# Tiles of 128 rows for remainders in the second expert layer, and its first tile's first layer placed at the end of the attention before it

## The chip, the core and the metric

The kernel runs on one core of one Trainium2 chip. The metric is the device time of one execution in microseconds; three executions are timed, and a further one is recorded by the profiler. All arithmetic is in 32-bit floats.

The engines are named as in the profile: PE is TensorE's matrix products and PEld its weight loads, DVE is VectorE, ACT is ScalarE, POOL is GpSimd, SP is SyncE, which here only issues transfers. Each engine works off its own queue in order.

## What is computed

Two decoder layers follow one another. Each has a cross-attention and a mixture of experts, and each result is added to its input. The part that matters here is the last step, the second mixture of experts:

```python
x = x + _L0_xattn_ref(...)
x = x + _L0_ffn_ref(...)
x = x + _L1_xattn_ref(ctx_1024, _layernorm(x), Wq, Wk, Wv, 1, 0, 1)
x = x + _L1_ffn_ref(_layernorm(x), W1, b1, W2, b2, Wr, br)

def _L1_ffn_ref(x, W1, b1, W2, b2, Wr, br):
    xf = x.reshape(-1, D)                    # 2048 rows of 256
    logits = xf @ Wr + br                    # 8 experts
    topv, _ = lax.top_k(logits, 2)
    masked = jnp.where(logits >= topv[:, 1:2], logits, -jnp.inf)
    weights = jax.nn.softmax(masked, axis=-1)
    h = gelu(jnp.einsum('td,edh->eth', xf, W1) + b1[:, None, :])   # 256 -> 1024
    expert_out = jnp.einsum('eth,ehd->etd', h, W2) + b2[:, None, :]  # 1024 -> 256
    return jnp.einsum('etd,te->td', expert_out, weights)
```

Each of the 2048 rows (4 batches of 512) has a weight of zero for all but its two best experts, so the kernel computes only those 4096 pairs of row and expert.

## The kernel before

The kernel gathers the rows of each expert and works on them in tiles of `G` = 256 rows, `GR` = 2 blocks of `P` = 128. A row that has been routed is scattered, together with its number and its weights (`PAY` = 265 values), into a table in DRAM. There are two such tables. `rows_a` has exactly 256 places for each expert and takes rows of the first three batches; `rows_b` takes what overflows there, and all rows of the last batch. Which rows fall to which expert is known only when the kernel runs. So the first eight tiles, one for each expert, come from `rows_a` at fixed addresses (`first_tile`, L1591). Further tiles come from `rows_b` by indirect gathers, whose indices the kernel works out itself (`table`, L1683; `further_tile`, L1750). `SURE` = 13 such tiles are always done. More of them, up to 21 in all, are written out behind conditions on a counter (`beyond`, L1826), and one of these is fetched in advance.

**A tile.** `turned` (L1613) transposes the 256 rows on TensorE into `tp` and copies them to `xT` with VectorE. `hidden` (L1623) is the first layer: 16 products of 128 by 128 by 256 in four groups, each group followed by two GELUs on ScalarE into `hT`. `second` (L1647) and `results` (L1673) are the second layer: for each block of 128 rows 8 products into `ps_y`, a multiplication by the row's weight on VectorE into `y`, and an indirect add into the output in DRAM by GpSimd (`add_out`, L1661). `told` (L1570) reads from the gathered rows where each row goes (`to`) and its weight (`share`). The tiles `to`, `share` and `y` come from the pool `five`, which has five buffers of each; a sixth use waits until the add that reads the first is done. In the profile each product of 32-bit floats shows as two records.

**The order of tiles.** The loop at L1801 does `hidden` of tile i, fetches tile i + 2, does `turned` and `told` of tile i + 1, then `results` of tile i - 1. Between these it takes steps of `rest`, a generator that routes the last batch (`route2`, L396) and then works out the tables. These are the source's order only: in this stage a scheduler at build time decides the order on each engine. The weights of an expert are 4104 values for each partition, 2052 KB. There are four places for them, chosen by `room` (L1579): the large tile `cw`, the pool `new`, and two buffers of the pool `kv1`.

**Before that stage** comes the second cross-attention, which has 16 units of 13 tiles of keys each, in steps of two tiles. There `in_order` fixes the order of the source on every computing engine, and a table `at`, filled by `put`, says which other work is issued at which step. `closing` (L1396) ends a unit: copy of the result `oT`, row sums over the adds `sum` (`ps_n`, then the copy `by`), transposes (`tp_o`), and the add into `x`. In the last batch the routing of the third batch runs beside it, with its scatters into `rows_a` and `rows_b` on GpSimd. `load_first_weights` (L1448) fetches the weights of tiles 0, 1 and 2 in this stage; `cw` takes those of tile 2. The pools of the expert stage reuse the memory of the attention's, so its first operations wait for the attention's last ones, the scatters included.

The lines that the loop and the places of weights rest on:

```python
        def room(k):
            if k % 4 == 2:
                return cw[:, :WIDE]
            if k % 4 == 3:
                return new.tile([P, WIDE], F32, tag="w", name="w_e")
            return kv1.tile([P, KV], F32, tag="kv", name="w_e")[:, :WIDE]
```

Of the kernel before, what the change touches and what calls it, by code (L numbers as in the profile page):

```python
# [8 lines left out]
F32 = mybir.dt.float32  # L9
# [7 lines left out]
P = 128  # L17
# [39 lines left out]
SURE = 13  # L57
# [13 lines left out]
def xattn_ffn_twice(ctx: ExitStack, tc: tile.TileContext, a: dict, out: bass.AP):  # L71
# [1243 lines left out]


# [3 lines left out]
    with ExitStack() as st:  # L1320
# [127 lines left out]
        def load_first_weights():  # L1448
# [11 lines left out]
            nc.sync.dma_start(cw[:, :WIDE], a["wall"][2 * P : 3 * P, :])  # L1460
# [6 lines left out]
            first_weights.append(lambda i, n: cw[:, i : i + n])  # L1467
# [44 lines left out]
        put(per_batch * (B - 1) + 4, load_first_weights)  # L1512

# [44 lines left out]
    with ExitStack() as st:  # L1558
# [4 lines left out]
        five = st.enter_context(tc.tile_pool(name="d_five", bufs=5))  # L1563
# [6 lines left out]
        def told(rows, share_of):  # L1570

            to = five.tile([P, GR], I32, tag="to", name="to")
            share = five.tile([P, GR], F32, tag="share", name="share")
            for r in range(GR):
                nc.vector.tensor_copy(to[:, r : r + 1], rows[r][:, D : D + 1])
                share_of(share[:, r : r + 1], rows[r][:, D + 1 :])
            return rows, to, share

        def room(k):  # L1579


            if k % 4 == 2:
                return cw[:, :WIDE]
            if k % 4 == 3:
                return new.tile([P, WIDE], F32, tag="w", name="w_e")
            return kv1.tile([P, KV], F32, tag="kv", name="w_e")[:, :WIDE]
# [4 lines left out]
        def first_tile(e):  # L1591

            rows = []
            for r in range(GR):
                got = three.tile([P, PAY], F32, tag=f"rows{r}", name=f"rows{r}")
                nc.sync.dma_start(got, rows_a[e * G + r * P : e * G + (r + 1) * P, :])
                rows.append(got)
# [15 lines left out]
        def turned(rows, two=two):  # L1613

            xT = two.tile([P, DC, G], F32, tag="xT2", name="xT2")
            tp = ps_t.tile([P, DC, GR, P], F32, tag="t", name="tp2")
            for c in range(DC):
                for r in range(GR):
                    nc.tensor.transpose(tp[:, c, r, :], rows[r][:, c * P : (c + 1) * P], ident)
            nc.vector.tensor_copy(xT, tp.rearrange("p c r q -> p c (r q)"))  # L1620
            return xT

        def hidden(w, xT, two=two):  # L1623

            hT = two.tile([P, FC, G], F32, tag="hT2", name="hT2")
            for f0 in range(0, FC, 2):
                ps = ps_h.tile([P, 2, G], F32, tag="h", name="ps_h2")
                for f in range(2):
                    for c in range(DC):
                        at = c * FF + (f0 + f) * P  # L1630
                        nc.tensor.matmul(  # L1631
                            ps[:, f, :],
                            lhsT=w(at, P),
                            rhs=xT[:, c, :],
                            start=c == 0,
                            stop=c == DC - 1,
                        )
                for f in range(2):
                    nc.scalar.activation(
                        hT[:, f0 + f, :],  # L1640
                        ps[:, f, :],
                        AF.Gelu,
                        bias=w(WB2 + f0 + f, 1),
                    )
            return hT
# [27 lines left out]
        def results(w, to, share, hT, n=T):  # L1673
            for r in range(GR):
                ps = second(w, hT, r)
                y = five.tile([P, D], F32, tag=f"y{r}", name=f"y{r}")
# [6 lines left out]
        def table():  # L1683
# [3 lines left out]
            for k, t in enumerate((taken2, taken_a)):  # L1687
# [5 lines left out]
            counts = one.tile([P, 2], F32, name="counts")  # L1693
            nc.vector.tensor_reduce(counts[:, 1:], ps_x, AX.X, ALU.add)
# [4 lines left out]
            nc.vector.tensor_tensor(rest, count[:, 0, :], skip, ALU.subtract)  # L1699
            steps = one.tile([P, E, T // G], F32, name="steps")  # L1700
            nc.vector.tensor_tensor(
                steps, bc(rest, [P, E, T // G], 2), bc(full, [P, E, T // G], 1), ALU.is_gt
# [3 lines left out]
            upto = one.tile([P, E], F32, name="upto")  # L1706
            sums = one.tile([P, E, E], F32, name="sums")
            nc.vector.tensor_tensor(sums, bc(tiles, [P, E, E], 1), notafter, ALU.mult)
            nc.vector.tensor_reduce(upto, sums, AX.X, ALU.add)
            nc.vector.tensor_copy(counts[:, :1], upto[:, E - 1 :])  # L1710
            yield
            past = one.tile([P, NG, E], F32, name="past")
            nc.vector.tensor_tensor(
                past, bc(number, [P, NG, E], 2), bc(upto, [P, NG, E], 1), ALU.is_ge
            )
            which = one.tile([P, NG], F32, name="which")
            nc.vector.tensor_reduce(which, past, AX.X, ALU.add)
            w_at = one.tile([P, NG], F32, name="w_at")
            w_idx = one.tile([P, NG], I32, name="w_idx")
            nc.vector.tensor_scalar(w_at, which, float(E - 1), float(P), ALU.min, ALU.mult)  # L1720
            nc.vector.tensor_scalar(w_at, w_at, lane[:, 0:1], None, ALU.add)
            nc.vector.tensor_copy(w_idx, w_at)
            mine = one.tile([P, NG, E], F32, name="mine2")
            nc.vector.tensor_scalar(mine, past, -1.0, 1.0, ALU.mult, ALU.add)
            nc.vector.tensor_tensor(mine[:, :, 1:], mine[:, :, 1:], past[:, :, : E - 1], ALU.mult)
            yield

            spent = one.tile([P, NG, E], F32, name="spent")
            x_at = one.tile([P, NG], F32, name="x_at")
            nc.vector.tensor_tensor(spent, past, bc(tiles, [P, NG, E], 1), ALU.mult)  # L1730
            nc.vector.tensor_reduce(x_at, spent, AX.X, ALU.add)
            nc.vector.tensor_tensor(x_at, number, x_at, ALU.subtract)
            held = one.tile([P, NG], F32, name="held")
            nc.vector.tensor_scalar(held, which, float(E), float(G), ALU.is_lt, ALU.mult)
            nc.vector.tensor_tensor(x_at, x_at, held, ALU.mult)
            nc.vector.tensor_tensor(spent, mine, bc(skip, [P, NG, E], 1), ALU.mult)
            nc.vector.tensor_reduce(held, spent, AX.X, ALU.add)
            nc.vector.tensor_tensor(x_at, x_at, held, ALU.add)
            nc.vector.scalar_tensor_tensor(x_at, which, float(PLACES), x_at, ALU.mult, ALU.add)
            nc.vector.tensor_scalar(x_at, x_at, lane[:, 0:1], None, ALU.add)  # L1740
            x_idx = one.tile([P, GR, NG], I32, name="x_idx")
            nc.vector.tensor_copy(x_idx[:, 0, :], x_at)
            for r in range(1, GR):
                nc.vector.tensor_scalar(x_at, x_at, float(P), None, ALU.add)
                nc.vector.tensor_copy(x_idx[:, r, :], x_at)
            state.update(mine=mine, w_idx=w_idx, x_idx=x_idx, counts=counts)
# [3 lines left out]
        def further_tile(i, k, three=three):  # L1750

            rows = []
            for r in range(GR):
# [6 lines left out]
                        ap=state["x_idx"][:, r, i : i + 1], axis=0  # L1760
# [10 lines left out]
                in_offset=bass.IndirectOffsetOnAxis(ap=state["w_idx"][:, i : i + 1], axis=0),  # L1771
# [4 lines left out]
            def share_of(to, weights):  # L1776
                of = two.tile([P, E], F32, tag="told", name="told")
                nc.vector.tensor_tensor(of, weights, state["mine"][:, i, :], ALU.mult)
# [13 lines left out]
        more += [lambda i=i: further_tile(i, E + i) for i in range(SURE)]  # L1792
        more.append(lambda: further_tile(SURE, E + SURE, spare))

        def ready(w, rows, share_of):
            return (w, turned(rows), *told(rows, share_of)[1:])

        last = None
        next(rest)
        here = ready(*fetched.pop(0))  # L1800
        for i in range(E + SURE):  # L1801
            w, xT, to, share = here
            hT = hidden(w, xT)
            for _ in range(2):
                next(rest, None)
            if more:
                fetched.append(more.pop(0)())
            if i + 1 < E + SURE:
                here = ready(*fetched.pop(0))
# [5 lines left out]
            if i == E + SURE - 3:  # L1815

                counts_i = one.tile([P, 2], I32, name="counts_i")
# [3 lines left out]


        n_tiles = nc.values_load(counts_i[0:1, 0:1], min_val=0, max_val=NG)
        ties = nc.values_load(counts_i[0:1, 1:2], min_val=0, max_val=E * T)

        def beyond(i, fetched=None):  # L1826
            with tc.If(n_tiles > i):
                w, xT, to, share = ready(*(fetched or further_tile(i, 2 + i % 2)))
                results(w, to, share, hidden(w, xT))
                if i + 1 < NG:  # L1830
                    beyond(i + 1)

        assert (E + SURE) % 4 < 2
# [111 lines left out]
```

## Time and profile before

| quantity | value |
| --- | --- |
| three timed executions | 2949.18, 2953.87, 2956.38 us; median 2953.87 us |
| profiled execution, its own time | 2949.11 us |
| profiled execution, span in the trace | 2947.0 us |
| mean granted TensorE clock | 0.973 |
| tile of 256 rows, in the steady part of the expert stage | 32 records `ps_h` at L1631 (6.88 us of weight loads), 32 records `ps_y` at L1650 (6.78 us) |
| last product of the stage begins | 2929.9 us after the span's start |
| last add into the output is issued | 2933.33 us |
| indirect load of one expert's weights, from issue to landing | 9.0 us (11 of them), 2052 KB |
| indirect gather of 128 rows, issue to landing | 3.0 us |
| indirect add of 128 rows into the output, issue to landing | 4.3 us |

The page divides the span into 40 slices of about 74 us. The upper line is TensorE's busy share in tenths, the middle one its granted clock in tenths, the lower one GpSimd's busy share:

```profile
PE   6999999999999999999999799988989898889997
PEclk9999999999999999999999899999999999999999
POOL 0000000100001000010000101021314233333442
```

The expert stage is the last five slices. The seam between attention and experts, at about 2600 us, is at the end of the 36th slice and shows as an 8 for TensorE only as a mean over it. In a chain of waits or a timeline, each row gives the start in microseconds from the span's start, the duration in microseconds, then the engine, the tile that is written (in the timeline also what is read) and the line; `x32` counts merged instructions, and a bracket at the end says how long the engine stood idle before and what ended that.

### The profile page before, as it was taken

How to read it: one execution, taken by the hardware profiler on the slowest of the kernel's cores; microseconds unless marked ns; L12 is line 12 of the kernel's file. 1: busy time of each engine (PE TensorE's matmuls, PEld its weight loads, DVE VectorE, ACT ScalarE, POOL GpSimd, SP SyncE). 2: the span in 40 equal slices, each digit the busy share in tenths (PEclk: the TensorE clock that was granted, in tenths of full speed). 3: DMA queues.
4: the chain of work that ended last, by engine and by line, in shares of the span. 5: the costliest groups of instructions: out<-in, count | busy, mean ns of one | idle time of the engine just before them, and what ended most of it. 6: DMA issues, size and time to landing. Idle time of an engine off the chain costs nothing. (4 is left out here: it accounts for less than half of the span.)

```text
span 2947.0 us, 36216 instructions
## 1 busy us (share of the span) xinstructions
PE 2770.3 (94%) x13686; PEld 1883.4 (64%) x13686; DVE 1466.2 (50%) x2333; ACT 937.7 (32%) x1325; POOL 392.5 (13%) x301
## 2 busy tenths in 40 slices
PE   6999999999999999999999799988989898889997
PEld 2666667666766666666666587744444444467886
DVE  6445456544575544454444202267767768742110
ACT  3323334233342333332332112134434344331221
POOL 0000000100001000010000101021314233333442
PEclk9999999999999999999999899999999999999999
DMA  5444443343434333343346798610101021035663
GB/s 162 113 108 113 104 112 85 102 106 92 104 98 109 95 91 92 89 109 94 91 99 185 199 255 235 185 46 16 30 28 48 19 66 63 11 114 154 180 188 82
DMA packets 197448, 314.94 MB, mean 107 GB/s; under 512 B 44007, under 2 KB 118056, under 8 KB 194440
## 3 DMA queue, kind: packets, MB, share of 16 engines
q1 hardware_dynamic: 157512, 227.52, 29.1%
q0 software_dynamic: 15168, 49.23, 5.7%
q10 hardware_dynamic: 24576, 35.68, 4.7%
q8 instruction: 114, 1.87, 0.3%
q14 instruction: 78, 0.64, 0.1%
HBM read 114.64 MB, written 51.86 MB: 56 GB/s over the span
## 5 line engine op out<-in xcount | busy, mean ns | idle before, releaser
L806 DVE TENSOR_REDUCE top<-ps_s 128x1 f32<-128x2113 f32 x128 | 301.9, 2358 | 585.2 <-PE ps_s L798 585.2
L835 PE MATMUL ps_o<-pT,v 128*128 128x256 f32 x2176 | 521.1, 381 | 0.5 <-DVE inv L813 0.5
L798 PE MATMUL ps_s<-kT,qT 128*128 128x512 f32 (+1 forms) x1280 | 488.8, 526 | 6.5 <-ACT attn L812 6.4
L835 PEld LDWEIGHTS ps_o<-pT,v 128*128 128x128 f32 x2176 | 410.0, 191 | 114.5 <-issue 68.3
L812 ACT ACTIVATE attn<-ps_s,top 128x2113 f32<-128x2113 f32 x128 | 258.9, 2023 | 477.5 <-DVE top L806 433.2
L798 PEld LDWEIGHTS ps_s<-kT,qT 128*128 128x128 f32 x1280 | 241.8, 191 | 252.9 <-issue 236.5
L827 DVE STREAM_TRANSPOSE pT<-swapped 128x2176 f32<-128x2176 f32 x128 | 312.4, 2441 | 31.0 <-DMA swapped<-attn 20.4
L1120 DVE TENSOR_REDUCE tops<-ps_s 128x2 f32<-128x1024 f32 (+1 forms) x224 | 238.1, 1105 | 149.6 <-PE ps_s L1109 149.2
L747 PE MATMUL ps_k<-kvin,wkv 128*128 128x512 f32 (+1 forms) x640 | 263.8, 535 | 4.1 <-DVE mv_g L685 2.1
L1357 PE MATMUL ps_w<-asked,keyed 64*128 64x256 f32 (+1 forms) x1664 | 244.7, 416 | 21.1 <-DVE tops L1120 9.6
L781 PE MATMUL ps_v<-wkv,kvin 128*128 128x256 f32 x1088 | 254.6, 381 | 0.7 <-ACT v L788 0.6
L1357 PEld LDWEIGHTS ps_w<-asked,keyed 64*128 64x128 f32 (+1 forms) x1664 | 147.5, 190 | 146.6 <-ACT pT L1370 61.8
L1370 ACT ACTIVATE pT<-ps_w 128x1024 f32<-128x1024 f32 (+1 forms) x176 | 179.3, 1023 | 193.7 <-PE ps_w L1357 191.9
L781 PEld LDWEIGHTS ps_v<-wkv,kvin 128*128 128x128 f32 x1088 | 205.0, 190 | 35.9 <-ACT v L788 6.0
L1379 DVE TENSOR_TENSOR sum<-sum,pT 128x1024 f32<-128x1024 f32 (+1 forms) x128 | 183.2, 1431 | 10.4 <-ACT pT L1370 4.0
L760 ACT ACTIVATE kT<-ps_k,bqk 128x512 f32<-128x512 f32 (+1 forms) x160 | 96.8, 620 | 266.5 <-DMA swapped<-attn 129.0
L1379 POOL TENSOR_TENSOR sum<-sum,pT 128x1024 f32<-128x1024 f32 x48 | 122.6, 2554 | 347.5 <-ACT pT L1370 347.3
L747 PEld LDWEIGHTS ps_k<-kvin,wkv 128*128 128x128 f32 x640 | 116.4, 192 | 78.5 <-issue 67.4
L1109 PE MATMUL ps_s<-kv,qT 32*128 32x512 f32 (+1 forms) x1024 | 135.4, 574 | 14.6 <-ACT kv L1013 6.5
L788 ACT COPY v<-ps_v 128x512 f32<-128x512 f32 x144 | 79.7, 560 | 217.0 <-PE ps_v L781 150.2
L1193 PE MATMUL ps_h<-sxT,w 128*128 128x256 f32 x512 | 116.7, 386 | 2.9 <-ACT hT L1200 2.1
L1207 PE MATMUL ps_y<-w,hT 128*128 128x256 f32 x512 | 114.4, 380 | 0.2 <-DVE y L1215 0.2
(282 smaller groups left out, 2731.5 us busy)
## 6 DMA issues: line engine op xcount, KB each, us to landing
swapped<-attn SPq DMA_DIRECT2D x1536, 68.0 KB, 2.1
swapped<-attn ACTq DMA_DIRECT2D x512, 68.0 KB, 2.2
w<-in_w_dram SPq DMA_DIRECT2D x32, 1024.0 KB, 10.2
rows_b<-empty SPq DMA_DIRECT2D x36, 530.0 KB, 11.3
w_e<-in_wall_dram SPq DMA_DIRECT2D x4, 2052.0 KB, 9.3
cw<-in_ctxT_dram SPq DMA_DIRECT2D x4, 1601.0 KB, 12.5
keyed<-kv SPq DMA_DIRECT2D x32, 200.1 KB, 3.8
ctx_b<-in_ctx_dram SPq DMA_DIRECT2D x3, 1536.0 KB, 8.0
```

The lines of the kernel that those rows point to most:

```text
L747: nc.tensor.matmul(ps[:, :n], lhsT=wkv[:, c, hs], rhs=kvin[:, c, : NB - 1, k, :] if k < 4 else kvin[:, c, NB - 1, :, :], start=c == 0, sto ...
L781: nc.tensor.matmul(ps[:, k, :], lhsT=flat_kvin[c][:, j * P : (j + 1) * P], rhs=wkv[:, c, cols], start=c == 0, stop=c == DC - 1,)
L798: nc.tensor.matmul(flat[:, j0 : j0 + n], lhsT=qT[:, t * P : (t + 1) * P], rhs=kT[:, j0 : j0 + n], start=True, stop=True,)
L806: nc.vector.tensor_reduce(top, flat[:, :L], AX.X, ALU.max, negate=True)
L812: nc.scalar.activation(attn[:, :L], flat[:, :L], AF.Exp, bias=top, accum_out=total)
L827: nc.vector.transpose(pT[:, :, k * P : (k + 1) * P].rearrange("p c (a i) -> p a c i", a=4), swapped.rearrange("p a (c i) -> p a c i", i=32),)
L835: nc.tensor.matmul(ps, lhsT=v[:, j - parts[part][0], (h % 2) * DH0 : (h % 2 + 1) * DH0], rhs=pT[:, j, :], start=j == 0, stop=j == NB - 1,)
L1109: nc.tensor.matmul(pss[i // 2][:, i % 2, at : at + n], lhsT=qTs[b][rows, o, q0 : q0 + P], rhs=kvs[b][0][o][rows, j0 : j0 + n], start=True, ...
L1120: nc.vector.tensor_reduce(tops[u][:, t : t + at // n, 2 * pair : 2 * pair + 2, j0 // 512], of, AX.X, ALU.max,)
L1357: nc.tensor.matmul(ps[:r, s, pair * QH : (pair + 1) * QH], lhsT=keyed[o][64 * s : 64 * s + 64, pair, j * P : j * P + r], rhs=asked[u % 3][ ...
L1370: nc.scalar.activation(pT[:r], ps[:r], AF.Exp)
L1379: (nc.gpsimd if k else nc.vector).tensor_tensor(to, to, pT[:r], ALU.add)
```

## The change

1. **Short tiles.** A remainder of an expert's rows of at most 128 is done as a tile of one block. `SURE` becomes a list: nine long tiles and four short ones, always done, in a fixed pattern. `table` counts long and short tiles apart and works out indices for each kind; `turned`, `hidden` and `results` take the number of rows from their operands, so that a short tile has half of the transposes, products of the first layer with 128 moving columns instead of 256, and one block of the second layer.
2. **The first tile.** Its rows and those of tile 1 are fetched by SP at the attention's step `NM * n_units - 6` into a part of `cw`; the rows of tile 0 are transposed at step -2, and the first layer is done in two halves at steps +2 and +5, counted from the end of the last unit's products. The loop then begins with tile 0's first layer done. `cw` no longer holds tile 2's weights, which are fetched at the start of the expert stage instead, into another place; `room` is turned to fit.
3. **Buffers.** The pool for `to`, `share` and `y` has eight buffers instead of five.
4. **The end.** The tile fetched in advance is gone. One counter tells whether anything is left over, further long or short tiles or ties, and one condition stands around all that follows.

```diff
-SURE = 13
+SURE = [True, True, False] * 3 + [True, True, True, False]
+SURE_LONG = sum(SURE)
+SURE_SHORT = len(SURE) - SURE_LONG
...
+    def turned_rows(rows, xT, tp):
+        for c in range(DC):
+            for r, some in enumerate(rows):
+                nc.tensor.transpose(tp[:, c, r, :], some[:, c * P : (c + 1) * P], ident)
+        nc.vector.tensor_copy(xT, tp.rearrange("p c r q -> p c (r q)"))
+
+    def hidden_some(w, xT, hT, f0, ps):
+        n = xT.shape[-1]
+        for f in range(2):
+            for c in range(DC):
+                at = c * FF + (f0 + f) * P
+                nc.tensor.matmul(ps[:, f, :n], lhsT=w(at, P), rhs=xT[:, c, :],
+                                 start=c == 0, stop=c == DC - 1)
+        for f in range(2):
+            nc.scalar.activation(
+                hT[:, f0 + f, :], ps[:, f, :n], AF.Gelu, bias=w(WB2 + f0 + f, 1)
+            )
...
             nc.sync.dma_start(t[:, :WIDE], a["wall"][P : 2 * P, :])
-            nc.sync.dma_start(cw[:, :WIDE], a["wall"][2 * P : 3 * P, :])
...
-            first_weights.append(lambda i, n: cw[:, i : i + n])
+
+        first_rows = []
+        first_h = cw[:, : FC * G].rearrange("p (f q) -> p f q", f=FC)
+        first_x = cw[:, FC * G : (FC + DC) * G].rearrange("p (c q) -> p c q", c=DC)
+
+        def load_first_rows():
+            for r in range(2 * GR):
+                at = (FC + DC) * G + r * PAY
+                got = cw[:, at : at + PAY]
+                nc.sync.dma_start(got, rows_a[r * P : (r + 1) * P, :])
+                first_rows.append(got)
+
+        def turn_first():
+            ps = ps_s.tile([P, DC, GR, P], F32, tag="s", name="tp_f")
+            turned_rows(first_rows[:GR], first_x, ps)
+
+        def first_layer(fs):
+            for f0 in fs:
+                ps = ps_s.tile([P, 2, 512], F32, tag="s", name="ps_f")
+                hidden_some(first_weights[0], first_x, first_h, f0, ps)
...
         put(per_batch * (B - 1) + 4, load_first_weights)
+        put(NM * n_units - 6, load_first_rows)
+        put(NM * n_units - 2, turn_first)
+        put(NM * n_units + 2, lambda: first_layer(range(0, FC // 2, 2)))
+        put(NM * n_units + 5, lambda: first_layer(range(FC // 2, FC, 2)))
...
-        five = st.enter_context(tc.tile_pool(name="d_five", bufs=5))
+        eight = st.enter_context(tc.tile_pool(name="d_eight", bufs=8))
...
         def room(k):
+            if k % 4 == 0:
+                return cw[:, :WIDE]
             if k % 4 == 2:
-                return cw[:, :WIDE]
-            if k % 4 == 3:
                 return new.tile([P, WIDE], F32, tag="w", name="w_e")
             return kv1.tile([P, KV], F32, tag="kv", name="w_e")[:, :WIDE]
...
         def first_tile(e):
-            rows = []
-            for r in range(GR):
+            rows = first_rows[e * GR : (e + 1) * GR]
+            for r in range(len(rows), GR):
...
         def results(w, to, share, hT, n=T):
-            for r in range(GR):
+            for r in range(hT.shape[-1] // P):
                 ps = second(w, hT, r)
-                y = five.tile([P, D], F32, tag=f"y{r}", name=f"y{r}")
+                y = eight.tile([P, D], F32, tag=f"y{r}", name=f"y{r}")
...
             steps = one.tile([P, E, T // G], F32, name="steps")
+            beyond_p = one.tile([P, E], F32, name="beyond_p")
+            nc.vector.tensor_scalar(beyond_p, rest, -float(P), None, ALU.add)
             nc.vector.tensor_tensor(
-                steps, bc(rest, [P, E, T // G], 2), bc(full, [P, E, T // G], 1), ALU.is_gt
+                steps, bc(beyond_p, [P, E, T // G], 2), bc(full, [P, E, T // G], 1), ALU.is_gt
             )
             tiles = one.tile([P, E], F32, name="tiles")
             nc.vector.tensor_reduce(tiles, steps, AX.X, ALU.add)
+            behind = one.tile([P, E], F32, name="behind")
+            nc.vector.scalar_tensor_tensor(behind, tiles, float(G), skip, ALU.mult, ALU.add)
+            short = one.tile([P, E], F32, name="short")
+            nc.vector.tensor_tensor(short, count[:, 0, :], behind, ALU.is_gt)
             yield
+            for k, (of, n, width, places) in enumerate(
+                ((tiles, NG, GR, skip), (short, E, 1, behind))
+            ):
...
-        def further_tile(i, k, three=three):
-            rows = []
-            for r in range(GR):
+        def further_tile(i, k, long):
+            mine, w_idx, x_idx = state[long]
+            rows = []
+            for r in range(GR if long else 1):
...
-        more += [lambda i=i: further_tile(i, E + i) for i in range(SURE)]
-        more.append(lambda: further_tile(SURE, E + SURE, spare))
+        for k, long in enumerate(SURE):
+            i = sum(long == other for other in SURE[:k])
+            more.append(lambda i=i, k=k, long=long: further_tile(i, E + k, long))
...
         last = None
+        w, rows, share_of = fetched.pop(0)
+        here = (w, None, *told(rows, share_of))
         next(rest)
-        here = ready(*fetched.pop(0))
-        for i in range(E + SURE):
+        for i in range(n):
             w, xT, to, share = here
-            hT = hidden(w, xT)
-            for _ in range(2):
+            hT = hidden(w, xT) if i else first_h
+            for _ in range(3):
                 next(rest, None)
...
-        n_tiles = nc.values_load(counts_i[0:1, 0:1], min_val=0, max_val=NG)
-        ties = nc.values_load(counts_i[0:1, 1:2], min_val=0, max_val=E * T)
...
-        assert (E + SURE) % 4 < 2
-        beyond(SURE, fetched.pop())
-        with tc.If(ties > 0):
...
+        with tc.If(count_of(0, 2 + E * T) > 0):
+            beyond(count_of(1, NG), SURE_LONG, NG, True)
+            beyond(count_of(2, E), SURE_SHORT, E, False)
+            with tc.If(count_of(3, E * T) > 0):
+                ties()
```

In the part that is left out, the loop over `k` in `table` holds for each kind of tile what the old code did for the one kind. On the engines' queues the built program shows these differences besides: GpSimd adds tile 0's results before it scatters the last batch's rows, where the old order put four scatters first; the second layer of tile 0 stands on TensorE ahead of the routing's transposes; and the table has 51 VectorE operations instead of 29. Up to the attention's last unit each engine's order of work is the same, apart from the load of `cw` that is gone.

## The prediction, made before the changed kernel had run

> **What bounds the kernel now.** I read the page's engine shares first, then the chain of waits over the last 350 us, then that stretch's timeline.
>
> ```profile
> PE 2770.3 (94%) x13686; PEld 1883.4 (64%) x13686; DVE 1466.2 (50%) x2333; ACT 937.7 (32%) x1325; POOL 392.5 (13%) x301
> ```
>
> TensorE is busy 94% of the span, but that is a mean over stages; only the seam from attention to experts and the expert stage behind it (2596 to 2947 us) are edited. The chain of waits there (start, duration, engine, tile, line):
>
> ```profile
> 2605.40 2.59 DMA rows_b<-pay,place_b
> ...
> 2608.98 2.73 DMA rows<-rows_a
> ...
> 2612.71 9.02 PE ps_h L1631 x32
> ...
> 2626.26 2.59 PE ps_h L1631 x12
> ...
> 2658.55 8.10 DMA out_dram<-y,to
> ...
> 2667.42 3.71 DMA out_dram<-y,to
> 2671.23 0.21 DVE to L1575 x2
> 2671.44 0.61 DVE xT L1620
> 2672.09 0.61 PE ps_x L1690 x2
> 2672.70 8.78 PE ps_y L1650 x28
> 2681.49 6.91 PE ps_h L1631 x32
> 2688.39 0.44 PE tp L1619 x4
> 2688.83 6.91 PE ps_y L1650 x32
> ```
>
> Three regimes. (a) To 2626: scatters, row loads, then tile 0's first layer (9.02 us), during which nothing else advances. (b) Until 2672 the chain runs over GpSimd's scatters and adds into `out`, and through a VectorE cast to a `to` buffer: `five` has 5 buffers, so tile 5's `to` waits for tile 0's adds. (c) From 2681.49 it is TensorE alone: 6.91 + 0.44 + 6.91 = 14.26 us for each 256-row tile, to the last product at 2930.25. The timeline shows the stall of (b), and what 128 columns cost:
>
> ```profile
> 2664.03 1.11 PE L1650 MATMUL ps_y<-cw,hT 128*128 128x256 f32 x4
> 2667.42 1.56 POOL L1663 DMA_INDIRECT out_dram<-y,to  x1 [7.31 <-DMA out_dram<-y,to]
> 2671.23 0.21 DVE L1575 CAST to<-rows 128x1 int32<-128x1 f32 x2 [13.97 <-DMA out_dram<-y,to]
> ```
> ```profile
> 2602.72 1.88 PE L1407 MATMUL ps_n<-sum,ones 128*32 128x256 f32 x16 [4.27 <-DVE sum L1379]
> 2623.45 1.85 PE L424 MATMUL ps_l<-wr,xnT 128*128 128x8 f32 x16
> ```
> ```profile
> 711.50 0.61 PE L747 MATMUL ps_k<-kvin,wkv 128*128 128x128 f32 x4
> ```
>
> VectorE stood 13.97 us before that cast; the copies and `y` products queued behind it held TensorE from 2665.1 to 2672.1. Attention ends with another hole, 4.27 us before `ps_n`.
>
> **What the Trainium skill says.** "TensorE: Matmul & The Clock Gate", section "LDWEIGHTS": a weight load costs by its columns, 128/1.2 = 107 ns, however few the moving columns. The trace agrees: 16 records of 8 columns take 1.85 us, 116 ns each, though a load alone is listed at 190. The same page, "What's actually happening": after an idle window of some 3.4 us the array runs at half clock. It agrees: the windows view gives clock 0.50 from 2606 to 2616, and the 28 records after the stall took 8.78 us, 314 ns each, instead of 216. "DMA: Bandwidth & Descriptors", "Anatomy of one DMA": 2.0 us + bytes/436e3; 2.10 MB would be 6.8 us (estimate). The trace says 9.0 for the indirect weight load, which I use.
>
> **Does the change do what it says?** Before, the remainders behind the first 256 rows of each expert make 13 tiles. The reference's own routing of its inputs (top 2 of `logits`, all rows less min(256, rows of the first three batches)) leaves 38, 145, 87, 516, 646, 176, 380, 181 rows: ceil(n/256) sums to 13, the old `SURE`. With the new rule (long tiles = ceil((n-128)/256), short if rows are left) it is 9 long and 4 short, exactly the new list. So four tiles shrink and no conditional tile runs.
>
> **Part 1, short tiles.** A product is two records. First layer: 32 records of 256 columns, 6.91 us. At 128 columns the K-projection rows give (0.61 - 0.27 for the last one's latency)/3 = 0.113 us each, so 32 x 0.113 = 3.6; saves 3.3. Second layer: one block of rows instead of two, 16 x 0.216 = 3.45 saved. Two transposes fewer: 0.22. Together 7.0 us, times 4 = 28.0, all on the path of (c). Behind it: the GELUs (2 in 0.84 us per pair, less at half width, against 0.9 of TensorE); the chained adds (4.3 us to landing, one per short tile of 7.2 us); the weight load, issued after the second layer four tiles back, with 28.5 us before its first use and 21.5 when one tile between is short, against 9.0. These hide. Bounds: loads at the listed 190 ns would leave 6.1 us for the first layer (save 0.8: 18 in all); a pace of 107 gives 29. I take 28.
>
> **Part 2, the seam.** Moved: four row loads on SP (8 took 4.41 us; SP's queue is empty from 2545 to 2608, so nothing waits behind them). They wait for the last `rows_a` scatter, issued 2576.5, and are needed near 2594: about 10 us of slack. Four transposes (0.44) go before the last `ps_o` products, which wait for ScalarE anyway. The `xT` copy (0.69) goes on VectorE before the last two `sum` adds and pushes `ps_n` by 0.7. The first 16 records (3.45) fit the 4.27 us hole; the second 16 (3.45) stand between `ps_n` and `tp_o` on TensorE. The GELU table load (1.28) and eight GELUs stand around `by`, hidden. I work out `x` complete at 2609.9 instead of 2607.5. But the routing's statistics started only at 2608.86, held by the `rows_b` scatters; so they lose about 1.4 us.
>
> Then, without the 9.02: tile 0's second layer fills TensorE from 2609 while VectorE normalises; `pay` ready about 2616, logits 2619, tile 1's first layer from 2620.5 instead of 2626.1 (-5.6), and 26 second-layer records (26 x 0.216 = 5.6) are done by then that the old order did later. Gain 11.2.
>
> `eight`: tile 5's `to` waits for nothing; the first reuse is tile 8's, behind tile 0's adds, which in the new order GpSimd issues before the scatters. That removes the 7.0 us hole and 28 x (0.314 - 0.216) = 2.7 of slow clock: 9.7. What is late next: the new cast for tile 8 waits for its gather, queued behind eight scatters and tile 2's adds; I get 2671-2673 against 2672 when VectorE wants to empty tile 3's first block, with about 7 us before TensorE needs that bank. The routing table grows from 29 to 51 small VectorE operations of 0.2 us (+4.4), beside tile 3's first and tile 2's second layer (13.8 us); uncovered it would cost 4.4. Tile 2's weights, loaded at 2408 before, now come at the seam ahead of tile 3's: due 9.0 after about 2611, needed at 2632; small row loads behind two large ones could hold the casts 0 to 4 us. I deduct 2.4 for bubbles: tile 4's first layer at about 2662.8 instead of 2681.3, 18.5 gained (bounds 11 and 21).
>
> **Part 3, the end.** One counter and one branch instead of two: GpSimd, last to finish, spent 2938.8 to 2941.2 on the second: 2.4 (0 to 3). Three trailing adds at 4.2 us each against products of 3.45, instead of four: 0.8.
>
> Sum: 28.0 + 18.5 + 2.4 + 0.8 = 49.7. The profiled execution took 2949.11 (span 2947.0), so it would take 2899.4. The median is 2953.87, 4.8 higher; less 49.7 that is 2904.
>
> **Rivals.**
> - The stall returns (GpSimd's gather in place of the adds, or the loads of tiles 2 to 4 colliding): for, a chain of eight scatters plus adds took 2632 to 2671; against, they now start about 6 us earlier. It gives back the 9.7: 2914.
> - Short tiles don't halve: for, listed loads of 190 ns, and 2.1 MB per 7 us tile; against, 8-column records at 116 ns and 9.0 against 21.5 us. It gives back 10: 2914. If the weight queue gets late too, half of the 28: 2918.
> - Slower: overflow. Should the run's counts exceed the list, `beyond` does each extra tile unoverlapped: two gathers 2.4 + 3.0, weights 1.0 + 9.0, transposes and copy 1.1, layers 6.9 + 0.9 + 6.9, final add 4.3, a branch about 4: some 39 us. One extra cancels most of the gain (2943, no measurable loss), two make 2982. It decides from the second extra tile on. Against: the counts above, 13 in agreement with the old list; expert 6 is 4 rows from needing another long tile, and rounding moves single rows.
>
> **Numbers.** Likeliest 0.74 at 2904; the stall back 0.13; short tiles not halved 0.09; overflow by one tile 0.01, by more 0.03. The range runs from the gain with its upper bounds (29 + 21 + 4 = 54, and a few us of spread between runs) at 2896 to 2918, past both first rivals. This measurement tells 0.3% (9 us) from no change: faster 0.96, same 0.01, slower 0.03.
>
> **What would show it.** In the profile after: first-layer groups of 128x128 near 0.113 us a record, four short tiles near 7.2 us; no VectorE wait for `out` of over 2 us near 2650; tile 4's first layer near 2663; `ps_n` without a 4 us hole. A GpSimd or weight wait on TensorE's path, or a conditional tile at the end, would prove me wrong.

## The result, and the profile after

The changed kernel took 2910.64 us (median of four executions, 2907.83 to 2911.16), against 2951.52 us for the kernel before (the three executions listed above and a fourth): a ratio of 0.9855, with a 95% interval of 0.9841 to 0.987, or 40.9 us less. The forecast was 2904 with a range of 2896 to 2918; 2910.64 lies between that 2904 and the 2914 of the forecast's first two rivals, so the number alone decides for none of them. The profiled execution took 2910.62 us, with a span of 2908.8 and a mean clock of 0.972.

The engine shares on the page of the changed kernel:

```profile
PE 2746.4 (94%) x13614; PEld 1860.1 (64%) x13614; DVE 1460.5 (50%) x2339; ACT 935.3 (32%) x1325; POOL 379.8 (13%) x290
```

TensorE has 72 records fewer: four short tiles, each with 16 second-layer records and two transposes fewer. So the change does what it says, and no conditional tile ran.

The timeline of TensorE at the seam, and in the steady part of the expert stage:

```profile
2602.08 2.00 PE L1387 MATMUL ps_w<-asked,keyed 64*128 64x256 f32 x16
2604.01 1.07 PE L1418 MATMUL ps_o<-pT,kv 128*32 128x256 f32 x16
2605.01 0.66 PE L1324 MATMUL tp_f<-ident,cw 128*128 128x128 f32 x4
2605.59 1.07 PE L1418 MATMUL ps_o<-pT,kv 128*32 128x256 f32 x16
2607.80 3.72 PE L1333 MATMUL ps_f<-cw,w_g 128*128 128x256 f32 x16 [1.13 <-DVE cw L1325]
2611.45 1.07 PE L1437 MATMUL ps_n<-sum,ones 128*32 128x256 f32 x16
2612.45 3.72 PE L1333 MATMUL ps_f<-cw,w_g 128*128 128x256 f32 x16
...
2669.47 7.07 PE L1333 MATMUL ps_h<-xT,cw 128*128 128x256 f32 x32
...
2760.24 3.73 PE L1333 MATMUL ps_h<-xT,w_e 128*128 128x128 f32 x32
2763.81 0.60 PE L1324 MATMUL tp<-ident,rows 128*128 128x128 f32 x4
...
2778.50 3.62 PE L1687 MATMUL ps_y<-w_e,hT 128*128 128x256 f32 x16
2781.95 7.07 PE L1333 MATMUL ps_h<-xT,cw 128*128 128x256 f32 x32
```

Tile 0's transposes `tp_f` stand between the last `ps_o` products, and its first layer (`ps_f`) fills the hole that stood before `ps_n`. Tile 4's first layer begins at 2669.47. A short tile's first layer takes 3.57 us until the next start (2763.81 - 2760.24), its second layer 3.45 (2781.95 - 2778.50).

One stretch of the timeline, several engines together, does not look as forecast:

```profile
2654.70 0.98 POOL L539 DMA_INDIRECT rows_b<-pay,place_b  x1 [1.93 <-DMA rows_b<-pay,place_b]
2654.78 0.33 SPq L1660 DMA_DIRECT2D w_e<-in_wall_dram  x1
2662.69 0.98 POOL L539 DMA_INDIRECT rows_b<-pay,place_b  x1 [7.01 <-DMA rows_b<-pay,place_b]
...
2668.53 1.56 POOL L1700 DMA_INDIRECT out_dram<-y,to  x1 [1.67 <-DMA out_dram<-y,to]
2669.70 0.33 SPq L1660 DMA_DIRECT2D w_e<-in_wall_dram  x1
2678.81 1.56 POOL L1700 DMA_INDIRECT out_dram<-y,to  x1 [8.72 <-DMA out_dram<-y,to]
...
2683.95 0.33 SPq L1660 DMA_DIRECT2D w_e<-in_wall_dram  x1
2685.23 1.08 POOL L1824 DMA_INDIRECT rows<-rows_b,x_idx  x1 [0.30 <-issue]
...
2693.55 0.15 DVE L1631 CAST to<-rows 128x1 int32<-128x1 f32 x1 [15.85 <-DMA rows<-rows_b,x_idx]
2694.22 0.87 DVE L1714 TENSOR_SCALAR y<-ps_y,share 128x256 f32<-128x256 f32 x2
2694.75 8.86 PE L1687 MATMUL ps_y<-cw,hT 128*128 128x256 f32 x32 [3.52 <-DVE y L1714]
```

VectorE stands 15.85 us before the cast for tile 8, whose gathered rows land only at 2693.5. Both of tile 3's `y` products wait behind it, so TensorE waits 3.52 us for a PSUM bank, and its next 32 records take 8.86 us instead of 7.07. The scatter, the add and the gather that land so late are each issued within 1.3 us of a weight load on SP (`SPq`): the scatter just before one, the add 1.2 us before one, the gather 1.3 us after one. These are the loads for tiles 5, 6 and 7.

**A measure that leaves the attention out.** The attention ahead of the edits doesn't start its end at the same time in every execution: the start of the last `ps_w` group (2594.58 before, 2602.08 here) serves below as a zero mark. From it to tile 4's first layer, from there to the end of the last product, from there to the span's end, and from the mark to the span's end (us):

| kernel | mark | to tile 4's first layer | to the last product's end | tail | mark to end |
| --- | --- | --- | --- | --- | --- |
| before | 2594.58 | 86.7 | 248.9 | 16.75 | 352.4 |
| changed | 2602.08 | 67.4 | 226.4 | 12.96 | 306.7 |

So behind the mark the change saves 45.7 us; 7.5 of it are lost ahead of the mark, where the computation is nearly the same. Each row of this table and the next is one profiled execution. Two kernels were profiled twice, and their times from the mark to the end differ by 1.0 and 0.7 us.

### The profile page after: what moved, and what is told of

The parts are those of the page before. It is cut to its first block, busy times and chain, and to the rows that moved or that the text cites. A ratio compares the mean times of both kernels' runs of the same rounds, so it can differ in the third digit from the quotient of the medians.

```text
span 2908.8 us, 36010 instructions
## 1 busy us (share of the span) xinstructions
PE 2746.4 (94%) x13614; PEld 1860.1 (64%) x13614; DVE 1460.5 (50%) x2339; ACT 935.3 (32%) x1325; POOL 379.8 (13%) x290
## 5 line engine op out<-in xcount | busy, mean ns | idle before, releaser
L1409 DVE TENSOR_TENSOR sum<-sum,pT 128x1024 f32<-128x1024 f32 (+1 forms) x128 | 183.0, 1430 | 10.3 <-ACT pT L1400 4.0
```

The costliest lines, as they stand in the source:

```text
L1409: (nc.gpsimd if k else nc.vector).tensor_tensor(to, to, pT[:r], ALU.add)
```

## Experiments

All kernels of this section compared by the same mark:

| run | median us | mark | to tile 4 | tail | mark to end |
| --- | --- | --- | --- | --- | --- |
| e1_five | 2914.96 | 2603.10 | 77.5 | 13.38 | 314.7 |
| e2_long | 2934.09 | 2592.23 | 68.6 | 14.18 | 335.8 |
| e3_unmoved | 2907.48 | 2599.79 | 74.3 | 13.13 | 308.3 |
| e4_told_late | 2908.00 | 2597.81 | 68.5 | 13.10 | 302.5 |
| e5_unmoved_late | 2906.86 | 2595.81 | 75.5 | 12.93 | 309.3 |
| e6_before_eight | 2941.91 | 2596.34 | 77.8 | 16.79 | 343.6 |
| e7_before_late | 2940.15 | 2600.52 | 76.7 | 16.48 | 342.1 |
| e8_all_late | 2900.63 | 2596.75 | 68.5 | 12.73 | 302.2 |
| e9_fewer_loads | 2909.64 | 2605.29 | 68.9 | 13.36 | 303.2 |
| e10_after_again | 2907.73 | 2604.97 | 67.6 | 13.33 | 307.7 |
| e11_all_late_again | 2906.15 | 2601.63 | 69.1 | 12.91 | 302.9 |

**Five buffers** (the changed kernel, part 3 undone).

```diff
-eight = st.enter_context(tc.tile_pool(name="d_eight", bufs=8))
+eight = st.enter_context(tc.tile_pool(name="d_eight", bufs=5))
```

> The changed kernel with five buffers again for `to`, `share` and `y` instead of eight. My theory (eight buffers are what freed VectorE, worth 9.7 us): the cast for tile 6 waits again for tile 1's adds into `out` (they land near 2677), and the `xT` copy and `y` products queued behind it hold TensorE before tile 4's first layer by some 8 us with 2 us of slow clock; the cast for tile 8 then stands behind tile 3's `y` and its wait (5.5 us in the changed kernel) goes. Net +4 to +10: 2915 to 2920. Rival (the seam alone brought the adds forward, so five buffers no longer hold anything, and they keep tile 8's cast out of the way): 2 to 5 us shorter than the changed kernel's 2910.6, 2905 to 2909.

Measured 2914.96 us (2908.09 to 2919.51), at the lower edge of the first theory's range; behind the mark 8.0 more than the changed kernel. In the timeline of this kernel:

```profile
2679.66 0.21 DVE L1631 CAST to<-rows 128x1 int32<-128x1 f32 x2 [16.31 <-DMA out_dram<-y,to]
2680.39 0.87 DVE L1714 TENSOR_SCALAR y<-ps_y,share 128x256 f32<-128x256 f32 x2
2680.57 10.02 PE L1333 MATMUL ps_h<-xT,cw 128*128 128x256 f32 x32 [9.56 <-issue]
```

The cast for tile 6 waits for tile 1's adds, and TensorE stands 9.56 us, then runs slowly: the first theory. The stall at tile 8 is gone in exchange. In the new order, too, five buffers would be too few.

**No short tiles** (part 1 undone, but for the longer table).

```diff
-SURE = [True, True, False] * 3 + [True, True, True, False]
+SURE = [True] * 13
...
-            nc.vector.tensor_scalar(beyond_p, rest, -float(P), None, ALU.add)
+            nc.vector.tensor_scalar(beyond_p, rest, 0.0, None, ALU.add)
```

> The changed kernel with all thirteen further tiles long (256 rows), the rest of the change kept. Theory: a short tile is worth 7.0 us, four 28.0: 2910.6 + 28.0 = 2938.6 (2936 to 2941), all behind tile 8's stall. Rival (loads of weights under 128 columns cost their listed 190 ns, or the weight queue limits short tiles): 18 us, 2929.

Measured 29.1 more behind the mark. Its mark came early (2592.23), and the medians are only 23.5 apart, between the two theories; the time behind the mark speaks for the first. Of the 29.1, 26.6 lie between tile 4's first layer and the last product, where the stall at tile 8 takes 1.4 less than in the changed kernel, so that the tiles themselves account for 28.0; 1.2 lie ahead of tile 4 in a slow clock (last section), and 1.2 in the tail. The tail is 14.18: a long last tile costs 1.2 us of adds there, and of the tail before (16.75) the other 2.6 are put down to the second counter, by subtraction.

**Tile 0's first layer back behind the attention** (the computing half of part 2 undone).

```diff
-        put(NM * n_units - 2, turn_first)
-        put(NM * n_units + 2, lambda: first_layer(range(0, FC // 2, 2)))
-        put(NM * n_units + 5, lambda: first_layer(range(FC // 2, FC, 2)))
...
-        w, rows, share_of = fetched.pop(0)
-        here = (w, None, *told(rows, share_of))
         next(rest)
+        here = ready(*fetched.pop(0))
...
-            hT = hidden(w, xT) if i else first_h
+            hT = hidden(w, xT)
```

> The changed kernel with tile 0's transposes and first layer back behind the attention (its early row loads, eight buffers and short tiles kept). Theory: the move is worth the 11.2 us that the prediction gave it: 2921.8. Rival (the cast for tile 8 comes from GpSimd's chain of scatters and adds, whose start does not hang on the move, so a later TensorE meets no stall there): 11.2 - 5.5 = 5.7, 2916.3, and no wait of VectorE for tile 8's rows on TensorE's path.

Measured 2907.48 us, not above the changed kernel's 2910.64, and only 1.6 more behind the mark. Neither number was right, but the rival's mechanism was: tile 4 begins 6.9 us later, and no wait of TensorE stands at tile 8: the rows for it land 88.6 us after the mark, and TensorE, later itself, wants the bank only at 95.9. As built, most of what the move gains at tile 4 is waited away at tile 8: 6.9 - 5.5 (the stall's cost, worked out below) leaves 1.4.

**Casts late.** Each tile's `to` casts get an order-only dependency on the last `y` product stated before them; nothing else changes.

```diff
+        def after_y(ins):
+            tc.add_manual_dep(
+                ins,
+                ys[-1].name,
...
-        def told(rows, share_of):
+        def told(rows, share_of, held=False):
...
                 nc.vector.tensor_copy(to[:, r : r + 1], some[:, D : D + 1])
+                if held and ys:
+                    after_y(nc.cur_bb.bb.instructions[-1])
...
                 nc.vector.tensor_scalar(y, ps, share[:, r : r + 1], None, ALU.mult)
+                ys.append(nc.cur_bb.bb.instructions[-1])
...
-                here = ready(*fetched.pop(0))
+                here = ready(*fetched.pop(0), held=True)
```

> The changed kernel with each tile's casts (`to`, `share`) kept behind the `y` products that the program states before them, so that tile 8's cast stands behind tile 5's `y` on VectorE. Theory (the 3.5 us hole before tile 4's second layer and the slow clock behind it, 5.5 us in all, come from tile 8's cast alone): 2905.1, no hole near 2691. Rival (another wait, of the weights of tiles 5 to 8 or of GpSimd's adds, stands right behind it): 2909 to 2911, with TensorE waiting elsewhere in that stretch.

Measured 302.5 from the mark, 4.2 less, and no wait of TensorE behind tile 1. The median (2908.00, 2902.08 to 2916.76) does not resolve it. Tile 8's rows also land early in this run, 83.0 us after the mark instead of 91.4, so it doesn't tell by itself whether the later cast or the earlier rows took the stall away; e11_all_late_again does (below).

**Unmoved and late**, the interaction of the last two (here all operations of `told` are held, not the casts alone).

> Tile 0's first layer back behind the attention, as in the earlier run, and all of each tile's small operations on its rows (`to`, `told`, `share`) kept behind the `y` products stated before them. Counted from the last `ps_w` product of the attention to the span's end, since the attention ahead of it varies from run to run (the changed kernel 306.7, unmoved 308.3, casts late 302.5). Theory (the move is worth about 7 us as long as no stall follows it; the stall of tile 8's cast took 5.5 of them back): 308 to 310, the same as unmoved, 6 to 7 more than with casts late alone. Rival (the move is worth next to nothing on any path, and the unmoved kernel still held a stall that the late casts now remove): 302 to 304.

309.3, the first theory: the late casts give nothing where the layer isn't moved, and the move is worth 7.1 (309.3 - 302.2) where no stall takes it back.

**Before with eight buffers**, and **before with late operations and five buffers**.

```diff
-five = st.enter_context(tc.tile_pool(name="d_five", bufs=5))
+eight = st.enter_context(tc.tile_pool(name="d_eight", bufs=8))
```

> The kernel before with eight buffers instead of five for `to`, `share` and `y`, nothing else. Theory (the wait of VectorE for tile 0's adds was the stall of before, 7.0 us of hole and 2.7 of slow clock, and with the first layer unmoved TensorE is too late to meet tile 8's cast): 9.7 less, 342.7 from the last `ps_w` product to the span's end instead of 352.4. Rival (the same GpSimd chain then holds tile 8's cast, as in the changed kernel): 347 to 352.

343.6, 8.9 less than before, all of it gained by tile 4 (77.8 against 86.7): the first theory.

> The kernel before with its five buffers, each tile's small operations on its rows kept behind the `y` products stated before them; nothing else. Theory (not the number of buffers but the place of the casts in VectorE's order made the stall): the same 9.7 less as with eight buffers, 341 to 344 from the last `ps_w` product to the span's end. Rival (five buffers still tie tile 5 to tile 0's adds wherever the cast stands): 348 to 352, with a VectorE wait for `out` near 2660 on TensorE's path.

342.1, 10.3 less, with a ratio of 0.995 (0.9934 to 0.9966) against 0.9961 (0.9942 to 0.9979) for eight buffers. Both are the first theory. The place of the casts on VectorE made the old stall; more buffers are one way round it, a later place is another that costs no memory.

**All operations late on the changed kernel, twice, and the changed kernel again.**

> The changed kernel with all of each tile's small operations on its rows kept behind the `y` products stated before them (the earlier run kept the casts alone there). Theory: as with casts alone, 302 to 303 from the last `ps_w` product to the span's end, 4 us less than the changed kernel, no wait of TensorE of over 1.2 us behind the seam; as a median some 4 to 5 us below the changed kernel's 2910.6, within what runs vary. Rival (the operations on the rows, now late, hold the `y` products behind them somewhere else): 306 or more.

> The changed kernel unchanged, a second sample beside the late casts. Theory (its 7.5 us of delay ahead of the attention's end were spread between runs, the stall at tile 8 is not): the attention's last `ps_w` product anywhere from 2592 to 2603, 306 to 308 from there to the span's end, with TensorE waiting 3 to 4 us before tile 4's second layer. Rival (the stall is an accident of one run): 302 to 303.

> The changed kernel with all of each tile's small operations on its rows late, a second sample on the same chip as the changed kernel. Theory: 302 to 303 from the attention's last `ps_w` product to the span's end, and a median 4 to 5 us below the changed kernel's in the same rounds. Rival (the gain seen before was the luck of the attention's start): no lower median and 306 or more from the product.

Behind the mark: 302.2 and 302.9 late, 306.7 and 307.7 as changed; the changed kernel's second sample shows the stall again (3.96 us before 32 records of 8.86). Its mark, 2604.97, lies outside the 2592 to 2603 that was expected. In e11_all_late_again tile 8's gather is issued 2.0 us after the load of tile 7's weights and its rows land 93.3 us after the mark, later than in the changed kernel; still TensorE doesn't wait. So it is the late place of the casts that removes the stall. The same place in the timeline of e8_all_late:

```profile
2679.53 7.07 PE L1333 MATMUL ps_h<-xT,w_e 128*128 128x256 f32 x32
2686.43 0.60 PE L1324 MATMUL tp<-ident,rows 128*128 128x128 f32 x4
2686.87 7.07 PE L1704 MATMUL ps_y<-cw,hT 128*128 128x256 f32 x32
2693.78 7.07 PE L1333 MATMUL ps_h<-xT,w_e 128*128 128x256 f32 x32
```

TensorE goes from tile to tile without a gap. This is the best version found, by the trace. Whole executions don't confirm so small a gain: 2906.15 against 2907.73 in the same rounds, both at a ratio of 0.9828, where 4 to 5 us lower was expected. In these rounds the kernel before took 2958.75, so the changed kernel lies 51.0 us below it here and 40.9 in the first comparison.

**Fewer weight loads.** The kernel leaves out the loads for tiles 5, 6 and 7, which use weights that are already there; its output is not the reference's, and only its times are of use.

```diff
+            elif e >= 5:
+                w = kept[{5: 3, 6: 2, 7: 3}[e]]
             else:
...
-                w = columns(t)
+                w = kept[e] = columns(t)
```

> The changed kernel without the loads of the weights of tiles 5, 6 and 7 (each 2.1 MB on SP's queue): those tiles compute with the weights of tiles 3, 2 and 3, so their part of the sum is left wrong. Theory (the three long landings on GpSimd's chain, a scatter of 7.0 us, an add of 8.7 and tile 8's gather of 8.3, each lie behind one of these loads, and that is what makes tile 8's cast 14 us later than the prediction had it): the three shrink to about 2.7, 3.9 and 3, tile 8's gather lands some 75 to 78 us after the attention's last `ps_w` product instead of 91.5, TensorE meets no wait for the cast, and the span from that product ends at 301 to 303. Rival (scatters and adds into DRAM are slow in themselves where many are chained): the waits stay at 7 to 9 us, the stall stays, 306 to 307.

The timeline of this kernel, GpSimd and VectorE:

```profile
2659.47 0.98 POOL L539 DMA_INDIRECT rows_b<-pay,place_b  x1 [1.77 <-DMA rows_b<-pay,place_b]
2662.47 0.98 POOL L539 DMA_INDIRECT rows_b<-pay,place_b  x1 [2.02 <-DMA rows_b<-pay,place_b]
...
2670.34 1.06 POOL L1840 DMA_INDIRECT w_e<-in_wall_dram,w_idx  x1 [0.30 <-issue]
2673.02 1.58 POOL L1704 DMA_INDIRECT out_dram<-y,to  x1 [1.62 <-DMA out_dram<-y,to]
2680.62 1.55 POOL L1704 DMA_INDIRECT out_dram<-y,to  x1 [6.03 <-DMA out_dram<-y,to]
2682.48 1.07 POOL L1828 DMA_INDIRECT rows<-rows_b,x_idx  x1 [0.30 <-issue]
...
2685.51 0.15 DVE L1631 CAST to<-rows 128x1 int32<-128x1 f32 x1 [3.04 <-DMA rows<-rows_b,x_idx]
...
2687.04 0.47 DVE L1718 TENSOR_SCALAR y<-ps_y,share 128x256 f32<-128x256 f32 x1
2688.70 0.48 DVE L1718 TENSOR_SCALAR y<-ps_y,share 128x256 f32<-128x256 f32 x1 [1.18 <-PE ps_y L1691]
```

The scatter's wait fell from 7.01 to 2.02 and the gather lands 3.0 us after its issue instead of 8.3. One add still waited 6.03, and just there GpSimd had issued another weight load itself, that of tile 9, which found its place free early. So the rows came 80.2 us after the mark, 2 later than expected, still in time: of tile 3's two `y` products only the first stands behind the casts (2687.04), the second waits for TensorE, TensorE waits for neither, and the kernel ends 303.2 after the mark. The loads are what makes these links slow. That they also use the same engines is what the Trainium skill says ("DMA: Bandwidth & Descriptors", "Issuing engines are not separate DMA queues": transfers started by different engines run on the same 16 and interleave); the trace agrees, and adds that interleaving is no protection: 3.0 becomes 8.3 us for 128 gathered rows.

## Why the prediction came out so

The forecast, in the measure behind the mark, against the runs:

| term | forecast | measured | from |
| --- | --- | --- | --- |
| short tiles | 28.0 | 28.0 | tile 4's first layer to the last product: 248.9 before, 220.9 in e8_all_late |
| seam, up to tile 4 | 18.5 | 19.4 | 86.74 - 67.39 |
| stall at tile 8 | 0 | -5.5 | 226.4 - 220.9 |
| end | 3.2 | 3.8 | 16.75 - 12.96 |
| sum | 49.7 | 45.7 | |

- **Short tiles: right**, in the sum and in its parts (3.57 us for the first layer, where 3.6 was worked out from three records of the K projection, and 3.45 for the second). Nothing that was said to hide came out: no wait of TensorE stands in the steady part.
- **Eight buffers: right in mechanism and nearly in size**: 9.7 forecast, 8.9 by themselves on the old kernel (10.3 with late operations in their place; tile 0's first layer took 10.02 us in the one and 8.92 in the other, so about 1 us of these is no effect of the edits).
- **The moved layer: right up to tile 4.** 11.2 less 2.4 for bubbles makes 8.8; the step from e5_unmoved_late to e8_all_late is 6.9. Another 2.4 lie between e6_before_eight and e5_unmoved_late, which has the early row loads, but also the late operations and tile 2's weights in another place; so this share isn't separated. With the buffers' 8.9 these make 18.2; the other 1.1 of the 19.4 is a slow clock that the changed kernel's first profile happened not to have (last section), which is luck. Tile 1's first layer begins 27.0 us after the mark; the forecast's 2620.5 less 2594.58 is 25.9. `ps_n` came 9.4 after the mark instead of 8.1: 1.2 later, where 0.7 was charged.
- **Wrong: the step "the new cast for tile 8 waits for its gather, queued behind eight scatters and tile 2's adds; I get 2671-2673".** That is 76 to 78 us after the mark; the cast came at 91.5. The queue was the right one, but its landings were priced as if alone. Three of them were under way together with a weight load of 2.1 MB each, and cost 7.0, 8.7 and 8.3 us where the other links of the same kind cost about 2, 3 and 3: some 16 too many, against the 13 to 15 by which the cast was late. The forecast doesn't give its links one by one, so the two can't be matched exactly. TensorE wanted the bank at 2691.23 (2694.75 - 3.52), 89.2 after the mark, so 3.5 us of hole remained, and 1.8 of slow clock (8.86 - 7.07).
- So the rival **"The stall returns", named with GpSimd's gather**, is what happened, at the place it named, though with 5.5 us and not the 9.7 it gave. The forecast's argument against it, that the scatters and adds start about 6 us earlier, failed as well: the first of the last batch's scatters starts 36.9 us after the mark, against 38.0 before. The lines of before, and then of the changed kernel:

```profile
2632.56 0.98 POOL L535 DMA_INDIRECT rows_b<-pay,place_b  x1 [26.18 <-PE ps_h L1631]
```
```profile
2618.88 0.37 SPq L1660 DMA_DIRECT2D w_e<-in_wall_dram  x1
2620.24 0.71 SPq L1660 DMA_DIRECT2D w_e<-in_wall_dram  x1
2623.51 1.60 POOL L1700 DMA_INDIRECT out_dram<-y,to  x1 [8.24 <-issue]
2637.11 1.59 POOL L1700 DMA_INDIRECT out_dram<-y,to  x1 [11.99 <-DVE share L1665]
2639.00 1.03 POOL L539 DMA_INDIRECT rows_b<-pay,place_b  x1 [0.30 <-PE ps_h L1333]
```

The places for the scatters (`place_b`) were ready 33.0 us after the mark instead of 36.9. But tile 0's two adds stand ahead of the scatters now. The first landed only after 11.2 us, beside the loads for tiles 2 and 3, and the second had to wait for it: in all eight traces with the layer moved the first takes 10.7 to 11.3 us and the second starts 2.37 us after its landing, whatever its bracket names. One of these two loads, tile 2's, the change itself had moved to this place; the rival named the loads of tiles 2 to 4, too. No run takes these loads away, so that they are the cause here is argued from the loads of tiles 5 to 7, not shown.
- **The end: right**; 2.6 for the second counter, by subtraction (2.4 forecast), 1.2 for the shorter last tile (0.8).
- **In the range, but not in the sum: the spread of the attention.** The rest of the difference between 2904 and 2910.64, after the 4.0 of the sum, is 2.6 us, less than this spread.

**Where the 7.5 us ahead of the mark come from.** The timeline of the kernel before, and then that of the changed one, at the same unedited lines in the middle of the program:

```profile
1787.58 0.48 DVE L344 SCALAR_TENSOR_TENSOR x<-g,prob,x 128x256 f32<-128x256 f32 x1 [0.58 <-DMA g<-slot_y,slot]
...
1793.24 1.99 PE L1193 MATMUL ps_h<-sxT,w 128*128 128x256 f32 x8 [1.81 <-ACT hT L1200]
```
```profile
1790.43 0.48 DVE L348 SCALAR_TENSOR_TENSOR x<-g,prob,x 128x256 f32<-128x256 f32 x1 [2.70 <-DMA g<-slot_y,slot]
...
1795.80 3.78 PE L1197 MATMUL ps_h<-sxT,w 128*128 128x256 f32 x8 [3.77 <-ACT hT L1204]
```

A gather lands about 2 us later, TensorE's pause grows from 1.81 to 3.77 us, and the eight records behind it take 3.78 instead of 1.99 us; by 1802 the changed kernel's events come 5.2 us later than those of before, and near 1947 another 1.8 are lost to a slow clock (16 `ps_w` records in 3.79 instead of 2.00, behind a wait of only 0.47). The longer pause fits what the Trainium skill says ("TensorE: Matmul & The Clock Gate", section "What's actually happening"), that after an idle window of some 3.4 us the clock halves: the windows view gives 0.50 from 1795 to 1800. Whether the edits have a part in the 7.5 was not tried by itself. The marks show no clear one: three programs with the old attention order had 2594.58, 2596.34 and 2600.52, the ten traces of the changed kernel and its variants 2592.23 to 2605.29. The ranges overlap, and the spread within the ten is wider than the 7.5 us by which the two executions compared first lie apart.

## What to carry to other kernels

Price small transfers on a chain by what else is on the DMA engines at that moment: list the large loads due in the same stretch, and give each link that is under way beside one the longer landing, those at the head of the chain too. When a stall is removed from an in-order engine, look for the next instruction on that engine that waits for something unrelated to what stands behind it; putting it later in the order can do what more buffers do. And compare edits of under 0.3% from a mark just ahead of them, not by whole executions.

## What was not expected of the hardware

- **Clock dips without a long pause.** Tile 1's first layer starts after the same 0.78 us of waiting in all eight traces with the layer moved, yet its first 12 records took 2.86 us in three of them (the changed kernel, its repeat, five buffers) and 4.54 in the five others. The windows view of e8_all_late gives a clock of 0.77 from 2622 to 2626 there, that of the changed kernel 1.00 throughout. The other pauses ahead of it are as short (0.41 and 0.68 us). It moves about 1.2 us between runs, which is why tile 4 begins at 67.4 to 67.6 in two of them and at 68.5 to 69.1 in the others; what decides it stays open.
- **A long pause without a clock dip.** In e2_long TensorE waits 3.77 us before tile 4's second layer, as long as the pause at 1795 that halved the clock; the 32 records behind it take 7.17 us, at a clock of 1.00 from 2686 to 2694. In the changed kernel 3.52 us at the same place are followed by 8.86, at 0.70 from 2694 to 2698. So pauses of nearly one length cost 0.1 and 1.8 us here.
- **How much one load delays.** A scatter of 128 rows landed after 2.4 us at best, 2.6 in the middle and 7.7 at worst, an add after 3.8, 3.9 and 11.2, between 2600 and 2720 us of the changed kernel.
